# A four-layer image network: links of layer 0 on turns of their own, the scan's rows in bands, batch-norm statistics inside layer 2

## The chip, the cores and the metric

The program runs on one core of a Trainium2 chip. That core has four compute engines, each with its own in-order queue of instructions: PE (TensorE, matrix products into PSUM), DVE (VectorE), ACT (ScalarE) and POOL (GpSimd). A fifth queue, SP, issues every DMA of this kernel. The metric is the device time of one execution in microseconds; smaller is better. The profile shows, for PE, the clock that was granted as a share of the full one.

## The reference

Input `x` has 16 images of 64 x 64 positions and 256 channels, in float32. Four layers follow one another, each `x = x + layer(gn(x))`, where `gn` normalises each of 32 groups of 8 channels over an image. Layers 2 and 3 are involutions (weights made from the pixel, applied to its 3x3 or 7x7 surroundings); the change doesn't touch what they compute. Layers 0 and 1 are these:

```python
# layer 0: linear attention, 8 heads of 32
q, k, v = split(x @ Wqkv)
q = softmax(q, over the 32 of a head) / sqrt(32)
k = softmax(k, over all 4096 positions)
context = einsum('bdnh,benh->bdeh', k, v / 4096)
out = layernorm(einsum('bdeh,bdnh->benh', context, q) @ Wout + bout)

# layer 1: channel gate, then two spatial gates
xc = x * sigmoid(fc(mean(x)) + fc(max(x)))       # per image and channel
m  = mean of xc over channels, per position
y  = s6(m)         # h = exp(delta*A)*h + delta*m*B, y = sum(h*C), over 4096 positions
s  = conv7x7([mean, max of xc over channels])
x2 = xc * sigmoid(y) + xc * sigmoid(s)
out = relu((x2 - mean) / sqrt(var + eps) * gamma + beta)   # mean, var over all images
```

The last line is a batch norm: its mean and variance need all 16 images before any of them can go on.

## The kernel before

**Stages.** One function, `network`, writes the whole program; Python loops unroll all of it. Stage a is layer 0, with the gate and the channel maps of layer 1. Stage s holds layer 1's convolution, its scan, and its batch-norm statistics. Stage b is layer 2, stage c layer 3. Each stage opens pools of SBUF and PSUM buffers and closes them at its end, so that a later stage's buffers can lie where an earlier stage's were. Outside of a `manual_schedule` block, the framework chooses the order of instructions on each engine by the dependences and by the order in which they were written; inside one, they stay as written.

**Stage a.** It runs 256 turns and 16 more at the end. An image has 16 turns: two halves of four heads (`hf`), each with 8 chunks of 512 positions (`t`). In each turn, `attended` makes queries (pq, L280), and keys and values (pkv, L292), of one chunk on PE; ACT copies them out (L284, L301). Three kinds of further work are spread over the turns:

- For the half that was finished before: the context. `context` is a Python generator. Each `yield` ends a link, and `step()`, called five times in a turn, starts the next link. Links: the maximum of the keys over positions on DVE (mx, L311-L315), its transpose pk on PE (L331) and the diagonal matrix of it; the product pb that spreads the maximum over all partitions (L338), the subtraction on DVE (L341) and the exponential on ACT (L344); the product of keys and values pctx (L350, 128 small matmuls), scaled into cs.
- For the same half: the queries' softmax. `weighted` is a second generator. For each of two halves of the chunk range: maximum on DVE (L387), subtraction on POOL (L375), exponential on ACT (L380), sum and reciprocal on DVE (L383, L384), multiplication on POOL (L375 again). `output` then transposes queries (qT, L405), multiplies them with cs (po, L408) and transposes the result back (L409). `PARTS` says which of the eight outputs belong to which turn.
- For the image before: in the second half's turns, `projected0` (py, L423; bias, L428; squares on ACT, L432; the power on POOL, L435; transposes pt, L444; maxima and statistics, L451, L455). After an image's last chunk comes the gate `gate1`: group norm statistics (pg L134, pv L151, DVE L146-L148, the variance plus eps L93, POOL's power L94), av (L466-L469), ph (L477), hr and hs, pgate (L487), the sigmoid on ACT (L491), and the scale `ab` (L492-L494). `mapped` then takes the image two before: xm is scaled (ACT L172, DVE L175), transposed (px, L505) and reduced over channels on DVE (L509, L510).
- For the next image: `entered` takes statistics of the input (L246), and `norm0` makes from them the scale with which xn is normalised (ACT L165, DVE L166), half of the channels on each engine. A turn's pq needs its xn.

`norm0` and `gate1` are generators too, appended to `chains` in the turn in which their last chunk is done. py, pkv and px share a PSUM pool of two buffers; small products (pk, pb, pctx, pg, pv, ph, pgate) share one buffer.

**Stage s.** After the convolution (psc, L691), `r3` holds three rows for each image: delta, delta*m*m and delta*m, side by side for all images. The scan goes over 8 chunks of 512 positions with two groups of 8 images (16 steps). `rowed` transposes r3 (pr, L726) and ACT copies it (L731), for each chunk. `decayed` makes pa (L736): two matmuls over all 48 rows, against tables in which the rows of other images and of the other product are zero. ACT takes the exponential of one (L740), DVE scans (L749), PE sums over states (pys, L760), DVE writes y (L767, L768). Then the sigmoids are added to `fac`, which is transposed to rows (L777), copied to `held` (L778) and written to DRAM (`fac_d`, L779).

The statistics follow (L784-L800): for each of 128 tiles, x1 is loaded (L789, four buffers), PE spreads a row of `held` over the partitions (pf, L792), DVE computes z = (x1 - mean) * pf with a running sum (L797), and ACT squares z with a running sum (L801). Some 25 small operations (L805-L831) make `bnp` and rescale `ab`.

**Stage b.** Constants are loaded (L909-L917, and `folded` at L849), the padded tile `pad` is cleared on POOL (L923). Then a `manual_schedule` block runs 152 turns. In turns 0 to 127, `end_of_layer1` takes 512 positions of an image: x1 and pf are loaded again (L939, pf with a broadcast from `fac_d`), z is computed again (L970), ACT applies the norm and relu (L976), POOL adds x1 (L980), the sum is stored for later turns (L1208) and ACT squares it (L987). The projections start at turn 13, the involution at turn 21. A turn's loads are issued one turn ahead, and ahead of the stores of the turn before.

Of the kernel before, what the change touches and what calls it, by code (L numbers as in the profile page):

```python
# [15 lines left out]
P = 128  # L16
# [20 lines left out]
def network(ctx: ExitStack, tc: tile.TileContext, a: dict, out: bass.AP):  # L37
# [142 lines left out]
    with ExitStack() as st:  # L180
# [59 lines left out]
        def entered(i, ch):  # L240

            if ch == 0:
                st0[i] = wk.tile([P, 2, NCH, 6], F32, tag="st0", name="st0")
            xin = loaded.pop(("xin", i, ch))
            for h in range(2):
                nc.vector.bn_stats(st0[i][:, h, ch, :], xin[:, h])  # L246
            if i >= 2:
                stores.extend(halo.pop(0) for _ in range(min(3, len(halo))))
            if ch == NCH - 1:
                chains.append(norm0(i))  # L250
# [8 lines left out]
        normal = {}  # L259

# [57 lines left out]
        def context(i, hf):  # L318


            _, ka, va = qkv[i, hf]
            kf = ka.rearrange("p j d h -> p j (d h)")
            t = tree_max(
                lambda t: [kf[:, 8 * k : 8 * k + 8, :] for k in range(4)]
                + [t.rearrange("p (j e) -> p j e", e=P)],
                lambda t: [(t[:, 0:n], t[:, n : 2 * n]) for n in (512, 256, 128)],
            )
            yield
            yield
            pk = sm.tile([P, CT], F32, tag="sm", name="pk")  # L330
            nc.tensor.transpose(pk[:, 0:P], t[:, 0:P], ident)  # L331
            kmc = small.tile([P, 1], F32, tag="kmc", name="kmc")
            nc.vector.tensor_reduce(kmc, pk[:, 0:P], AX.X, ALU.max)
            diag = wk.tile([P, P], F32, tag="diag", name="diag")
            nc.vector.tensor_scalar(diag, ident, kmc, None, ALU.mult)
            yield
            pb = sm.tile([P, CT], F32, tag="sm", name="pb")
            nc.tensor.matmul(pb[:, 0:P], lhsT=ones, rhs=diag, start=True, stop=True)  # L338
            for jh in range(2):
                part = kf[:, jh * 16 : (jh + 1) * 16, :]  # L340
                nc.vector.tensor_tensor(  # L341
                    part, part, pb[:, 0:P].unsqueeze(1).broadcast_to([P, 16, P]), ALU.subtract
                )
                nc.scalar.activation(part, part, AF.Exp)  # L344
            yield
            yield
            pctx = sm.tile([P, CT], F32, tag="sm", name="pctx")
            for j in range(32):
                for h in range(4):
                    nc.tensor.matmul(  # L350
                        pctx[32 * h : 32 * h + 32, 0 : NB + 1],
                        lhsT=ka[:, j, :, h], rhs=va[:, j, :, h],
                        start=(j == 0), stop=(j == 31),
                    )
            rz = small.tile([P, 1], F32, tag="rz", name="rz")
            nc.vector.reciprocal(rz, pctx[:, NB : NB + 1])

            cs = wk.tile([P, P], F32, tag="cs", name="cs")
            nc.vector.scalar_tensor_tensor(
                cs.rearrange("p (h e) -> p h e", h=4),  # L360
                pctx[:, 0:NB].unsqueeze(1).broadcast_to([P, 4, NB]), rz,
                hmask.rearrange("p (h e) -> p h e", h=4), ALU.mult, ALU.mult,
            )
            ctx_m[i, hf] = cs

        def weighted(i, hf):
# [11 lines left out]

            def exponential(k):
                nc.scalar.activation(qa[:, halves[k]], qa[:, halves[k]], AF.Exp)  # L380
# [5 lines left out]
            for k in range(2):  # L386
                nc.vector.tensor_reduce(mq[:, halves[k]], qa[:, halves[k]], AX.X, ALU.max)  # L387
                scaled(k, mq, ALU.subtract)
                yield
            exponential(0)  # L390
            yield
            summed(0)
            exponential(1)
            yield
            scaled(0, mq, ALU.mult)
            summed(1)
            yield
            scaled(1, mq, ALU.mult)
            om[i, hf] = slots.tile([P, P, NB], F32, tag="slot", name="o")
# [13 lines left out]
        def projected0(i, ch):  # L413
# [45 lines left out]
            if ch == NCH - 1:  # L459
                chains.append(gate1(i))  # L460
# [83 lines left out]
        PARTS = ((), (), (), (0,), (1,), (2, 3), (4, 5), (6, 7))  # L544
        PARTS_LAST = ((), (), (), (0, 1), (2, 3, 4), (5, 6, 7), (), ())

# [7 lines left out]
        for ch in range(NCH):  # L554
# [4 lines left out]
            stores.clear()  # L559
        while chains:  # L560
# [4 lines left out]
        for n in range(LAST + 16):  # L565
# [6 lines left out]
            if t == 0 and 0 <= before[0] < NI:  # L572
                chains.append(context(*before))
            if t == 1 and 0 <= before[0] < NI:
                chains.append(weighted(*before))
# [55 lines left out]
    with ExitStack() as st:  # L631
# [4 lines left out]
        sm = st.enter_context(tc.tile_pool(name="s_sm", bufs=2, space=PSUM))  # L636

# [6 lines left out]
        bng = sconst("bng", [P, 2], a["bn_gamma"])  # L644
        bnb = sconst("bnb", [P, 2], a["bn_beta"])
# [4 lines left out]
        wrow = sconst("wrow", [3 * NI, NG, 2, P], a["wrow"].rearrange("k (g n s) -> k g n s", g=NG, n=2))  # L650
        wout = sconst("wout", [P, 16], a["wstate"])
        mv2 = sconst("mv2", [P, 2, 2, NI])
# [56 lines left out]
        r3 = sconst("r3", [P, NB, NI, 3])  # L709
        rd, rdmm, rdm = (r3[:, :, :, k].rearrange("p d i -> p i d") for k in range(3))  # L710
        nc.vector.scalar_tensor_tensor(rd, z, 0.0, az, ALU.max, ALU.add)
        nc.vector.tensor_tensor(rdm, rd, m, ALU.mult)
        nc.vector.tensor_tensor(rdmm, rdm, m, ALU.mult)
# [5 lines left out]
        with tc.manual_schedule():  # L719
# [3 lines left out]
            def rowed(ch):  # L723
                pr = tr.tile([P, CT], F32, tag="tr", name="pr")
                for q in range(4):
                    nc.tensor.transpose(  # L726
                        pr[0 : 3 * NI, q * P : (q + 1) * P],
                        r3[:, ch * 4 + q].rearrange("p i k -> p (i k)"), ident,
                    )
                rows[ch] = wk.tile([3 * NI, CT], F32, tag="rows", name="rows", bufs=2)  # L730
                nc.scalar.copy(rows[ch], pr[0 : 3 * NI, :])  # L731

            def decayed(ch, g):
                pa = mm.tile([P, 2, CT], F32, tag="mm", name="pa")
                for k in range(2):
                    nc.tensor.matmul(  # L736
                        pa[:, k], lhsT=wrow[:, g, k, :], rhs=rows[ch], start=True, stop=True
# [42 lines left out]
        facr = fac_d.rearrange("(i c) t -> i (c t)", i=NI)  # L780
# [3 lines left out]
        tot = sconst("tot", [P, 2, 2, NI, NCH])  # L784
        for i in range(NI):
            for ch in range(NCH):
                tk = slice(ch * CT, (ch + 1) * CT)
                x1 = wk.tile([P, 2, CT], F32, tag="x1", name="x1", bufs=4)
                nc.sync.dma_start(out=x1, in_=x1_d[i, :, :, tk].rearrange("h p t -> p h t"))  # L789
                pf = tr.tile([P, CT], F32, tag="tr", name="pf")  # L790
                row = i * NCH + ch
                nc.tensor.matmul(  # L792
                    pf, lhsT=ident[0:n, row : row + 1].broadcast_to([n, P]), rhs=held[0:n],
                    start=True, stop=True,
                )
                for h in range(2):
                    nc.vector.scalar_tensor_tensor(  # L797
                        x1[:, h], x1[:, h], ngm1[:, i, h : h + 1], pf, ALU.add, ALU.mult,
                        accum_out=tot[:, 0, h, i, ch : ch + 1],
                    )  # L800
                    nc.scalar.activation(  # L801
                        x1[:, h], x1[:, h], AF.Square, accum_out=tot[:, 1, h, i, ch : ch + 1]
                    )
        for k in range(2):
            nc.vector.tensor_reduce(mv2[:, :, k, :], tot[:, k], AX.X, ALU.add)  # L805
        nc.vector.tensor_scalar(mv2, mv2, 1.0 / NT, None, ALU.mult)
        sqm = sconst("sqm", [P, 2, NI])
        nc.vector.tensor_tensor(sqm, mv2[:, :, 0, :], mv2[:, :, 0, :], ALU.mult)
        nc.vector.tensor_tensor(mv2[:, :, 1, :], mv2[:, :, 1, :], sqm, ALU.subtract)
        for h in range(2):  # L810
            gate = ab[:, 0, :, h]
            nc.vector.tensor_tensor(mv2[:, h, 0], mv2[:, h, 0], gate, ALU.mult)
            nc.vector.tensor_tensor(mv2[:, h, 1], mv2[:, h, 1], gate, ALU.mult)
            nc.vector.tensor_tensor(mv2[:, h, 1], mv2[:, h, 1], gate, ALU.mult)


        mvb = sconst("mvb", [P, 2, 2])
        nc.vector.tensor_reduce(mvb[:, 0, :], mv2[:, :, 0, :], AX.X, ALU.add)
        nc.vector.tensor_scalar(mvb[:, 0, :], mvb[:, 0, :], 1.0 / NI, None, ALU.mult)
        dev = mv2[:, :, 0, :]  # L820
        for h in range(2):
            nc.vector.tensor_scalar(dev[:, h], dev[:, h], mvb[:, 0, h : h + 1], None, ALU.subtract)
        nc.vector.tensor_tensor(dev, dev, dev, ALU.mult)
        nc.vector.tensor_tensor(dev, dev, mv2[:, :, 1, :], ALU.add)
        nc.vector.tensor_reduce(mvb[:, 1, :], dev, AX.X, ALU.add)
# [832 lines left out]
```

## Time and profile before

| | |
|---|---|
| three runs | 8206.47, 8218.75 and 8226.33 us, median 8218.75 |
| the profiled execution | 8218.71 us |
| its span, first to last instruction | 8216.8 us |
| mean granted PE clock | 0.918 |
| PE, DVE, ACT, POOL busy | 6831.6, 5933.2, 4827.7, 3044.1 us |
| last pq of stage a starts | 2883.4 us |
| first psc of stage s starts | 3059.4 us |
| first and last scan start | 3074.5 and 3167.4 us |
| first statistic (L797) starts, last ends | 3176.5 and 3407.6 us |
| layer 2, turns 0, 1 and 8: z (L970) starts | 3416.8, 3429.8 and 3468.4 us |

A line of the profile by instruction gives: start and length in us, engine, line of the program, operation, output and inputs, sizes, and in brackets how long the engine had stood idle and what ended that. In a line by stretch, the pairs are busy time and number of instructions of PE, of PE's weight loads, DVE, ACT and POOL, then the granted clock, the busy share of the DMA engines and what they moved in GB/s. A matmul in float32 is two passes, each its own record. Turn lengths below are taken between the first pq of one turn and of the next; images 3 to 14 agree within some 4 us in 184.

### The profile page before, as it was taken

The numbers are of one execution on the slowest core, as the hardware profiler recorded it, in microseconds if no ns is written. First come the engines' busy times: TensorE is split into PE (matmuls) and PEld (weight loads), VectorE is DVE, ScalarE is ACT, GpSimd is POOL, SyncE is SP. The second block draws the span as 40 slices with busy tenths as digits, with TensorE's granted clock in tenths as the row PEclk, the third lists the DMA queues.
The fourth block names the chain that finished last, engine by engine and source line by source line (L and its number), as shares of the span: only waits on it lengthen the run. The fifth ranks groups of instructions, "written<-read, shape, count | busy, mean of one in ns | idle before, by whom it ended". The sixth has DMA issues, their size and how long they took to land. (4 is left out here: it accounts for less than half of the span.)

```text
span 8216.8 us, 213294 instructions
## 1 busy us (share of the span) xinstructions
PE 6831.6 (83%) x88348; PEld 5191.9 (63%) x88348; DVE 5933.2 (72%) x7071; ACT 4827.7 (59%) x11136; POOL 3044.1 (37%) x2154
## 2 busy tenths in 40 slices
PE   7888888888888867478888888888588888888897
PEld 5666666666666643156666666666477777777776
DVE  6787778787777775679999999999644444444444
ACT  3555555555555544676776767665455555555554
POOL 1222222222222210167888888887411212111112
PEclk9999999999999977798888888888799999999999
DMA  7644444344333334766777777775588888888887
GB/s 225 188 142 138 139 136 141 131 145 144 124 113 118 116 102 151 249 221 231 268 262 261 271 252 267 262 258 200 176 257 258 259 258 256 261 259 257 255 256 245
DMA packets 1079706, 1695.53 MB, mean 206 GB/s; under 512 B 136785, under 2 KB 682914, under 8 KB 1077586
## 3 DMA queue, kind: packets, MB, share of 16 engines
q1 hardware_dynamic: 1078738, 1681.89, 63.1%
q8 instruction: 696, 11.40, 0.6%
q14 instruction: 272, 2.23, 0.1%
HBM read 1234.54 MB, written 469.76 MB: 207 GB/s over the span
## 5 line engine op out<-in xcount | busy, mean ns | idle before, releaser
L1102 DVE TENSOR_TENSOR pd<-xs,pw 128x4608 f32<-128x4608 f32 x256 | 1261.2, 4946 | 1.4 <-ACT xs L1083 1.4
L1376 PE MATMUL pk<-rt,span 64*128 64x176 f32 x12288 | 1177.9, 328 | 52.6 <-issue 47.9
L1386 ACT ACTIVATE wm<-pk,spanb 128x176 f32<-128x176 f32 x2560 | 845.7, 424 | 573.4 <-PE pk L1376 570.3
L1115 POOL TENSOR_TENSOR pd<-pd 128x2048 f32<-128x2048 f32 (+2 forms) x384 | 1071.6, 2791 | 173.1 <-DVE pd L1102 82.7
L1462 POOL TENSOR_TENSOR ex<-ex,rx 128x192 f32<-128x192 f32 (+2 forms) x768 | 436.6, 570 | 1820.6 <-DVE ex L1455 1232.1
L1376 PEld LDWEIGHTS pk<-rt,span 64*128 64x128 f32 x12288 | 967.8, 191 | 132.8 <-issue 75.9
L1455 DVE SCALAR_TENSOR_TENSOR ex<-pa,msk,ex 128x192 f32<-128x192 f32 x704 | 294.3, 418 | 1006.5 <-ACT ex L1454 948.4
L292 PE MATMUL pkv<-wq,xn 128*128 128x256 f32 x4096 | 967.9, 382 | 14.4 <-ACT va L301 14.2
L1442 PE MATMUL pa<-wm,xw 126*32 126x48 f32 x45056 | 758.2, 214 | 220.9 <-issue 206.2
L375 POOL TENSOR_TENSOR qa<-qa,mq 128x1024 f32<-128x1024 f32 x256 | 507.4, 2005 | 1168.8 <-DVE mq L384 503.0
L1079 PE MATMUL pt<-ident,pad 128*128 128x128 f32 x4608 | 760.1, 327 | 214.8 <-ACT xs L1083 207.6
L1391 DVE TENSOR_TENSOR wm<-pk,spanb 128x704 f32<-128x704 f32 x896 | 794.2, 888 | 188.9 <-PE pk L1376 186.3
L292 PEld LDWEIGHTS pkv<-wq,xn 128*128 128x128 f32 x4096 | 771.3, 192 | 227.4 <-issue 101.1
L1442 PEld LDWEIGHTS pa<-wm,xw 126*32 126x32 f32 x45056 | 624.6, 111 | 403.1 <-issue 359.0
L1079 PEld LDWEIGHTS pt<-ident,pad 128*128 128x128 f32 x4608 | 623.6, 168 | 401.4 <-ACT xs L1083 265.5
L1083 ACT COPY xs<-pt 128x512 f32<-128x512 f32 x1152 | 608.0, 587 | 170.1 <-PE pt L1079 167.2
L1273 DVE TENSOR_REDUCE x<-pd 128x512 f32<-128x4608 f32 x128 | 634.0, 4953 | 4.4
L280 PE MATMUL pq<-xn,wq 128*128 128x512 f32 x1024 | 528.2, 631 | 91.2 <-DVE xn L166 74.0
L423 PE MATMUL py<-wo,o 128*128 128x256 f32 x2048 | 525.0, 412 | 31.4 <-DVE maps L510 27.6
L1454 ACT ACTIVATE ex<-pa,msk 128x192 f32<-128x192 f32 x704 | 299.2, 425 | 392.7 <-PE pa L1442 198.5
L423 PEld LDWEIGHTS py<-wo,o 128*128 128x128 f32 x2048 | 487.7, 310 | 63.9 <-issue 38.0
L1033 PE MATMUL px<-x2p,wis 128*128 128x512 f32 x1024 | 467.7, 599 | 12.8 <-DMA x2p<-x_d 8.1
(234 smaller groups left out, 11663.8 us busy)
## 6 DMA issues: line engine op xcount, KB each, us to landing
xw<-strips SPq DMA_DIRECT2D x1408, 256.0 KB
xn<-in_x SPq DMA_DIRECT2D x256, 512.0 KB
x_d<-x SPq DMA_DIRECT2D x256, 512.0 KB
strips<-cen SPq DMA_DIRECT2D x352, 256.0 KB
xin<-in_x SPq DMA_DIRECT2D x128, 512.0 KB
x<-in_x SPq DMA_DIRECT2D x128, 512.0 KB
xm<-x_d SPq DMA_DIRECT2D x128, 512.0 KB
x<-x_d SPq DMA_DIRECT2D x128, 512.0 KB
```

What stands on the lines that cost most here:

```text
L280: nc.tensor.matmul(pq, lhsT=wq[:, h, f0 : f0 + P], rhs=xn[:, h], start=(h == 0), stop=(h == 1),)
L292: nc.tensor.matmul(pkv[:, q], lhsT=xn[:, h, q * P : (q + 1) * P], rhs=wq[:, h, f0 + P : f0 + 384], start=(h == 0), stop=(h == 1),)
L423: nc.tensor.matmul(py[:, q, :], lhsT=om[i, hf][:, :, ch * 4 + q], rhs=wo[:, hf, :], start=(hf == 0), stop=(hf == 1),)
L1079: nc.tensor.transpose(pt[:, k, h * P : (h + 1) * P], lines[:, h, rc * 4 + e + k, 2 * j : 2 * j + P], ident,)
L1083: nc.scalar.copy(xs[:, e : e + 2, j, :], pt)
L1102: nc.vector.tensor_tensor(pd.rearrange("p r (g f) k -> p r g f k", f=16), run, pw.rearrange("p r (g k) -> p r g k", k=9).unsqueeze(3).broa ...
L1115: nc.gpsimd.tensor_tensor(pd[..., 0:n], pd[..., 0:n], pd[..., n : 2 * n], ALU.add)
L1273: nc.vector.tensor_reduce(x3[:, :, P:C], pd1, AX.X, ALU.add)
L1376: nc.tensor.matmul(pkv[:, b, m], lhsT=span[half, first + gg, s0 : s0 + P], rhs=rto[half, o // 4 * 2 + m, :], start=True, stop=True,)
L1386: nc.scalar.activation(dst[:, m // 2, m % 2], pkv[:, m // 2, m % 2], AF.Identity, bias=spanb[:, g0 + m : g0 + m + 1],)
L1391: nc.vector.tensor_tensor(dst, pkv, spanb[:, g0 : g0 + 4].rearrange("p (b m) -> p b m", b=2).unsqueeze(3).broadcast_to([P, 2, 2, NTL]), AL ...
L1442: nc.tensor.matmul(pav[p0 : p0 + 32, :, tj * TC : (tj + 1) * TC].rearrange("c g (w v) -> c g w v", v=2), lhsT=xw[0:TILE_IN, k, tj, 32 * q ...
```

## The change

Three parts. First, in layer 0, the links of `context` and `weighted` are no longer separated by a fixed number of `yield`s: a list says for each link at which step it runs, counted from the step in which its chain starts. `norm0` and `gate1` are put aside in `waiting` and start at turn 1 of the next half. `PARTS` leaves turn 3 without an output and gives turn 4 two. The last image's gate and the last half keep lists of their own.

```diff
@@ entered / projected0
-                chains.append(norm0(i))
+                waiting.append(norm0(i))
...
-                chains.append(gate1(i))
+                (waiting if i < NI - 1 else chains).append(gate1(i))
@@ new
+        def until(links):
+            at = 1
+            for step_no, link in links:
+                while at < step_no:
+                    yield
+                    at += 1
+                link()
@@ context: bodies of the links unchanged, each now a function
+            links = [maximum, diagonal, spread] + [
+                lambda jh=jh: exponential(jh) for jh in range(2)
+            ] + [product]
+            return until(zip(at, links))
@@ weighted
+            links = []
+            for f in (shifted, exponential, summed, lambda k: scaled(k, mq, ALU.mult)):
+                links += [lambda f=f, k=k: f(k) for k in range(2)]
+            order = sorted(range(8), key=lambda n: at[n])
+            return until([(at[n], links[n]) for n in order] + [(max(at), ended)])
@@ turns
-        PARTS = ((), (), (), (0,), (1,), (2, 3), (4, 5), (6, 7))
+        PARTS = ((), (), (), (), (0, 1), (2, 3), (4, 5), (6, 7))
+        CONTEXT, CONTEXT_LAST = (1, 5, 14, 14, 15, 19), (1, 3, 4, 4, 4, 7)
+        WEIGHTED, WEIGHTED_LAST = (1, 3, 5, 7, 11, 13, 12, 14), (1, 2, 3, 4, 4, 5, 5, 6)
...
-                chains.append(context(*before))
+                chains.append(context(*before, CONTEXT if n < LAST else CONTEXT_LAST))
             if t == 1 and 0 <= before[0] < NI:
-                chains.append(weighted(*before))
+                chains.append(weighted(*before, WEIGHTED if n < LAST else WEIGHTED_LAST))
+            if t == 1:
+                chains.extend(waiting)
+                waiting.clear()
```

In the old form the context's links ran at steps 1, 3, 4, 4, 4 and 6, and those of the queries at 1, 2, 3, 4, 4, 5, 5 and 6.

Second, the scan. `r3` becomes 128 columns wide for each block of positions: a band of 32 for each group of 8 images and each of the two products, cleared once and filled in part. Each matmul of pa reads its own band alone, 8 rows for the decay and 16 for the input.

```diff
+        r3 = pc.tile([P, NB, 2, 2, 32], F32, tag="r3", name="r3")
+        nc.gpsimd.memset(r3, 0.0)
...
-                        pr[0 : 3 * NI, q * P : (q + 1) * P],
-                        r3[:, ch * 4 + q].rearrange("p i k -> p (i k)"), ident,
+                        pr[:, q * P : (q + 1) * P],
+                        r3[:, ch * 4 + q].rearrange("p g k i -> p (g k i)"), ident,
...
+                    p0 = 64 * g + 32 * k
+                    band = slice(p0, p0 + 8 + 8 * k)
                     nc.tensor.matmul(
-                        pa[:, k], lhsT=wrow[:, g, k, :], rhs=rows[ch], start=True, stop=True
+                        pa[:, k], lhsT=wrow[band], rhs=rows[ch][band], start=True, stop=True
                     )
```

Third, the statistics leave stage s and become `batch_norm`, called first in stage b's `manual_schedule` block. It reads `held` back from `fac_d`, goes over images 1 to 15 and then image 0, and leaves image 0's x1 and z in the buffers of `xs` and `pd`, which layer 2 first uses at turn 20. Turns 0 to 7 of layer 2 then load nothing and compute no z. The tables for gamma and beta move to stage b's constants.

```diff
+        def batch_norm():
+            x1s = [spare(xs_p, [P, 6, 3, C], "xs") for _ in range(2)]
+            zs = [spare(pd_p, [P, 4, P, 9], "pd") for _ in range(2)]
...
+            nc.sync.dma_start(out=held, in_=fac_d)
+            todo = [(i, ch) for i in range(1, NI) for ch in range(NCH)]
+            todo += [(0, rc) for rc in range(NCH)]
+            def begin(k):
...
+                if i:
+                    tag = ("x3", "x2r")[k % 2]
+                    x1 = wk.tile([P, 2, CT], F32, tag=tag, name="x1", bufs=3)
...
+            for k in range(5):
+                begin(k)
+            for k, (i, ch) in enumerate(todo):
+                begin(k + 5)
...
@@ end_of_layer1
-            x1, pf = taken("x1"), taken("pf")
-            zs = [wk.tile([P, 2, 256], F32, tag="z", name="z", bufs=1), pf]
...
+            if i:
+                x1, pf = taken("x1"), taken("pf")
...
+            else:
+                x1, zs = (t.rearrange("p h (g t) -> p h g t", g=2) for t in kept.pop(rc))
@@ loads
-            if end:
+            if end and end[0]:
                 load_layer1(*end)
@@
         with tc.manual_schedule():
+            batch_norm()
             loads(0)
```

## The prediction

> **What bounds the kernel now.** I read first the busy times by stage, cut at each stage's first and last instruction.
>
> ```profile
> core 0: us, PE busy (x) PEld busy (x) DVE busy (x) ACT busy (x) POOL busy (x), PEclk, DMA share, GB/s
> 38.00:2884.00 2846.00, 2482.14 (x17611) 1887.91 (x17610) 2181.68 (x3213) 1627.15 (x2962) 643.24 (x426) 0.95 0.43 142
> 3059.00:3174.40 115.40, 105.16 (x249) 54.94 (x249) 33.11 (x69) 22.26 (x33) 0.00 (x0) 0.54 0.00 0
> 3174.40:3413.20 238.80, 156.54 (x256) 41.64 (x256) 184.21 (x537) 176.87 (x512) 0.70 (x2) 0.92 0.84 277
> 3413.20:3468.40 55.20, 0.00 (x0) 0.00 (x0) 15.49 (x25) 24.29 (x60) 28.04 (x18) 0.50 0.67 188
> ```
>
> Each line is a stretch, its length, each engine's busy time, the granted clock, the DMA engines' share and rate. Layer 0's 256 turns (line one) are 87% PE, with 364 us in which PE stands still. The scan (line two) is PE at 0.54 of its clock. Line three is the batch-norm statistics, with no engine full and DMA at 0.84; line four the first eight turns of layer 2. After 3468.4 us both programs have the same instructions in the same order on every engine, so only what lies before can change.
>
> Next, one image of layer 0 (16 turns, 183.4 us) by groups of turns: 0-2, 3-4, 5-7, 8-10, 11-15.
>
> ```profile
> 1417.60:1440.00 22.40, 19.07 (x72) 12.89 (x72) 22.40 (x32) 16.18 (x21) 6.54 (x4) 0.92 0.49 164
> 1440.00:1475.20 35.20, 22.23 (x341) 17.13 (x341) 29.29 (x58) 12.97 (x17) 9.34 (x7) 0.90 0.42 134
> 1475.20:1499.10 23.90, 23.59 (x98) 16.11 (x97) 19.55 (x26) 11.23 (x15) 1.81 (x1) 1.00 0.59 200
> 1499.10:1547.80 48.70, 42.52 (x417) 35.58 (x416) 40.84 (x46) 29.59 (x58) 17.20 (x12) 0.93 0.30 102
> 1547.80:1601.00 53.20, 52.06 (x222) 40.40 (x222) 32.36 (x56) 35.78 (x86) 6.93 (x7) 1.00 0.40 136
> ```
>
> Turns 5-7 and 11-15 are PE without a gap. PE loses 13.0 us in turns 3-4, 6.2 in 8-10, 3.3 in 0-2. PE's timeline says to whom:
>
> ```profile
> 1445.07 1.12 PE L280 MATMUL pq<-xn,wq 128*128 128x512 f32 x2 [3.90 <-DVE xn L166]
> 1450.93 3.27 PE L350 MATMUL pctx<-va,ka 128*32 128x33 f32 x183 [3.49 <-DVE isq L93]
> 1464.08 1.09 PE L505 MATMUL px<-ident,xm 128*128 128x128 f32 x8 [2.26 <-ACT xm L172]
> 1503.00 5.53 PE L423 MATMUL py<-wo,o 128*128 128x256 f32 x16 [2.02 <-DVE maps L510]
> 1517.32 0.33 PE L331 MATMUL pk<-ident,mx 128*128 128x128 f32 x1 [2.97 <-DVE mx L315]
> 1544.27 3.72 PE L423 MATMUL py<-wo,o 128*128 128x256 f32 x16
> ```
>
> It waits for VectorE each time (px for xm, whose scale comes from the gate). A stall costs twice: the same 16 passes took 5.53 us after one and 3.72 at the end of turn 10.
>
> **Layer 0, part by part.** No operation is added or removed; links move. In the order of instructions of the two built programs, turns 0-1 stand as before on all engines, except that PE's last item in turn 1 is the gate's pg instead of the contexts' pb.
>
> Half 0 (turns 0-7), on the clock above. Turn 2 starts at 1433.1 (before 1433.66) and PE runs pq and pkv to 1439.8. VectorE: kmc, diag and small ones to 1433.3, two query sums of 2.27 with a reciprocal of 0.54 and small ones to 1438.8. Then xn of turn 3 (0.54): it waits for POOL's multiply, as rows of L166 took 1.58 and of L175 2.14 beside one; 1440.4. Behind it the norm's dev, pv on PE to 1441.4, the variance at 1442. POOL's power stands between two multiplies of 1.95: 1443.7; the two av scalars wait out the second: 1446.2. ph, hr, two transposes (0.68), hs, pgate: 1448.5, where L487 was at 1459.8. PE then does pq of turn 4 (1.9) and pb, to 1450.8. The key subtraction, now here, is 2.24 twice on VectorE (1455.5), its exponential 1.91 on ACT; xm follows at 1456.0. What PE has left of turns 3-4 is px 1.0, pkv 3.7, the rest of pctx 4.2, px 1.0, pkv 1.85, po 1.9, pkv 1.85, px 1.0, together 16.7: turn 5 starts at 1472.7 against 1475.2, and takes 7.8 as turn 6 does, not 8.4. That is -3.1. PE has two gaps here, 1442.4-1446.3 and 1451-1456; if the passes after them run as slowly as the 5.53 row, 1.6 comes back. I take -1.5 (bounds +2, if every small VectorE item is held by POOL once more, and -5).
>
> Half 1. Turn 8 keeps its order and its 2.0 us wait. In turn 9 the order py x6, pk, py x2 puts 2.8 us of PE work where PE waited 2.97 for mx: mx is ready at 1516.4, py ends its six at 1516.8. That removes the wait and the slow py behind it (4.98 for 14 passes, 3.3 at the later rate): -4.6. In turn 10 pv stands second on PE, ahead of py, pkv, pt and pb; on VectorE it is behind the query sum (2.27), xn, a reciprocal and the maxima of x (0.69 each, up to 2.39 beside POOL): 1527.5, PE is there at 1526.0, so +1.6. pctx goes from turn 10 to the end of turn 11: pb at 1537.9, subtractions done by 1544.2, exponentials 1546.8, PE arrives at 1547.6, so no wait; the x normalisation that waits behind the subtractions is needed only a turn later. Two outputs in turn 12 instead of one each in 11 and 12 are the same work. Sum -3; the walk through all items gives -1.8; I take -2.5 (bounds +2, -6).
>
> So -4.0 us an image, times 14 images that have all the work: -56. In images 0 and 1 three halves show pctx waiting inside a turn (turns of 13.1 and 12.0 us between ones of 5 to 8); with pctx two turns after pb I count 4 each: -12. The last 16 turns keep their steps. Layer 0: -68 (bounds +44, -166).
>
> The Trainium skill, "TensorE: Matmul & The Clock Gate", Part 1, speaks against this change: after about 3.4 us without work the clock is halved, and comes back only after some 3.4 us of work. By that rule both gaps of half 0 would cost the full 1.7 us each; the sum would be 8136 instead of 8112.
>
> **Scan.** Before, a step's pa is four passes over 48 rows:
>
> ```profile
> 3104.60 0.58 ACT L731 COPY rows<-pr 48x512 f32<-48x512 f32 x1 [2.09 <-PE pr L726]
> 3105.23 3.78 PE L736 MATMUL pa<-rows,wrow 48*128 48x512 f32 x4 [0.67 <-ACT rows L731]
> 3108.93 1.89 PE L760 MATMUL pys<-wout,hst 128*128 128x16 f32 x8
> 6501.59 2.06 PE L1376 MATMUL pk<-rt,span 64*128 64x176 f32 x24
> ```
>
> PE is the loop: pa 3.78 + pys 1.89, and every second step 1.6 more for pr and its copy; 12.65 a pair. After, the two matmuls of pa use rows in different bands (8 and 16 rows, 32 apart). The last line is the nearest row: layer 3 alternates two 64-row bands; 24 passes of 176 columns in 2.06 us, where one after another they would need 24 x 176 x 0.43/512 = 3.5. So bands run side by side. Then pa is two passes long, 2.1, and a pair 9.7: 8 x 2.95 = 23.6. VectorE's loop (pys 1.89, ysc 0.46, scan 1.27, waits 0.2) is 3.8, just under PE's 4.0. The wider transposes and the six half-sized rd operations add some 0.6; the memset of r3 (4096 columns; L923 took 7.58 for 8976) has idle POOL for cover and would cost 3.5 without. I take -23 (bounds 0, if they don't overlap, and -35).
>
> In layer 3 PE goes from 32-column to 64-row tiles without a gap: 48 passes of L1442 end at 6501.67, L1376 starts at 6501.59. The Trainium skill, "TensorEngine Tiling (Array Packing)", Key Properties, says that a change of tiling mode drains TensorE; pa and pys alternate, 32 changes. By the row that is nothing; by the rule, with the 0.2 us by which a pass of L736 (1.05) outlasts the start of the next (0.85 on) as an estimate, the sum would rise by 6.
>
> **Statistics.** These are the same 256 VectorE and 256 ACT operations. Three things move.
>
> ```profile
> DVE x L797 <- DMA x<-x_d: 33.5, 57, 1.8
> SPq L789 <- ACT x L801: 170.9, 124, 3.9
> DVE z L970 <- DMA pf<-fac_d: 32.1, 8, 5.2
> ```
>
> (Who waited for whom: total us, times, longest.) First, the start. Before, four tiles lay loaded and the first operation ran at 3176.5. After, SP issues 17 constants first (15 took 10.2 us at 3413-3423, so 11.5), then reads held back from DRAM, then x1, which lands 3.5 us after issue (L222 at 1512.06, used at 1515.4): 3190.5, +14. Second, the loop: 128 tiles in 231 us, 1.80 each, with VectorE at 1.44 and DMA at 0.84. SP waited 171 us for a free one of four buffers; now there are six. Bounds 1.87 a tile (281 GB/s, none preloaded) and 1.57 (DMA share 1.0 at that rate); I take 1.76: -6. Third, the end. The constants, the memset of pad and image 0's loads no longer stand between the last statistic and layer 2: the first relu comes 5.6 us after it (before 10.1), and turns 0-7 go by ACT at 2 x (0.81+0.19) + 2 x (0.70+0.19) = 3.8 instead of 6.4. Turn 8's loads stand on SP behind the store of turn 5, and pf takes 6.6 from issue; its z comes at about +36.5 against +60.8: -24. Sum -16 (bounds -40, and +2 if pf also lands 4 us later).
>
> **Sum.** Against the profiled execution, 8218.7 (span 8216.8 and 1.9 around it; the median is 8218.75): 8218.7 - 68 - 23 - 16 = 8112.
>
> **Rivals.** (1) The gate's chain takes the freed place: in half 0 it and the contexts, now one behind the other, eat what the order saves, and half 1's pv wait does the same; layer 0 stays. For it: PE idles 9 us in turns 3-4 by my own walk. Against: the gate is done 11 us earlier. 8218.7 - 39 = 8180. (2) PE's queue is held by the norms: pv stands ahead of 16 us of free PE work in turn 10, and ahead of all of turn 3. For it: VectorE items of 0.1 us took 1.9 (L148) and maxima 2.39 beside POOL. At 5 us more at each pv, an image is 10 - 4 = 6 longer: 8218.7 + 84 - 12 - 39 = 8252, slower. It decides from 4.8 us net an image. (3) Layer 0's gaps close: of 22.5 us lost an image only 11 stay, 14 x 11.5 = 161 and 12: 8218.7 - 173 - 39 = 8007. Against: VectorE has 29 of 35 us in turns 3-4. (4) Bands don't overlap: 8135, a variant of the forecast.
>
> **Numbers.** Forecast with (4) 0.48, own range 8060 to 8165; (1) 0.20; (2) 0.17; (3) 0.15. A measurement of this kernel tells about 0.2%, 16 us. The forecast, (3) and two thirds of (1) are faster: 0.76; the rest of (1) and a little of (2) within: 0.09; slower 0.15. The range 8010 to 8230 leaves out half of (3) and most of (2).
>
> **What would show it.** The turns: 3-4 at some 33 us instead of 35.2 and 8-11 at 57 instead of 59.2; pk without a wait, pv with one of about 1.6, pctx in turn 11 without one; clock in turns 8-10 above 0.93. A scan pair of 9.7 us, with pa near 2.1. First statistic 14 us after the copy of held, 1.76 a tile, relus 3.8 us apart. I am wrong if turn 3's pq or turn 10's pv waits over 5 us, if pa stays 3.8, or if anything after layer 2's turn 8 changes its length.

## The result, and the profile after

The changed kernel takes 8111.56 us (median of 4 runs, 8107.73 to 8118.0) beside 8220.52 for the kernel before (4 runs, 8206.47 to 8226.33): ratio 0.987, 95% interval 0.9856 to 0.9883. The forecast of 8112 us was met by luck, not by its own sum. The two profiled executions, cut at the same events:

| stretch (us) | before | changed | difference | forecast |
|---|---|---|---|---|
| first to last pq of layer 0 | 2847.3 | 2852.1 | +4.9 | -68 |
| last pq to first psc | 174.7 | 171.8 | -2.9 | 0 |
| first psc to first scan | 15.1 | 14.3 | -0.8 | (in -23) |
| first scan to end of the copy of held | 99.8 | 75.8 | -24.0 | -23 |
| from there to the first statistic | 2.2 | 17.1 | +14.9 | +14 |
| 128 tiles of statistics | 231.1 | 174.4 | -56.6 | -6 |
| last statistic to the relu of layer 2's turn 8 | 61.6 | 33.5 | -28.1 | -24 |
| from there to layer 3's first pk | 2455.9 | 2455.1 | -0.8 | 0 |
| layer 3 | 2291.7 | 2275.8 | -15.9 | 0 |

Layer 0 gave nothing, and the loop of the statistics gave nine times what was put down for it. The stretches of the changed kernel, with the columns of the prediction's first fence:

```profile
38.00:2888.50 2850.50, 2515.81 (x17611) 1918.69 (x17610) 2134.87 (x3212) 1629.48 (x2961) 636.88 (x426) 0.94 0.43 142
3060.40:3150.90 90.50, 78.27 (x248) 46.20 (x248) 31.84 (x69) 22.20 (x33) 0.00 (x0) 0.56 0.00 0
3150.90:3168.00 17.10, 2.08 (x3) 1.08 (x4) 1.91 (x8) 0.01 (x1) 8.12 (x2) 0.50 0.38 113
3168.00:3342.50 174.50, 143.13 (x270) 41.22 (x269) 172.42 (x513) 171.37 (x509) 0.00 (x0) 0.99 1.02 379
3342.50:3348.80 6.30, 0.00 (x0) 0.00 (x0) 4.27 (x24) 1.02 (x5) 0.70 (x1) 0.50 0.00 0
3348.80:3375.10 26.30, 0.00 (x0) 0.00 (x0) 0.02 (x1) 23.51 (x60) 19.93 (x16) 0.50 0.48 170
```

Layer 0: PE is busy 33.7 us longer than before at a clock of 0.94 instead of 0.95, in a stretch 4.5 us longer. What the new order took away in idle time (334.7 us instead of 363.9) came back as slow passes. The statistics (fourth line) are now VectorE 172 of 174.5 us and ACT 171, with the DMA engines at 379 GB/s instead of 277 to 282. Turns 0 to 7 of layer 2 (last line) are set by ACT, busy for 23.5 of 26.3 us.

One image of layer 0 in the changed kernel, by groups of turns 0-2, 3-4, 5-7, 8-11, 12-15:

```profile
1424.60:1445.10 20.50, 17.50 (x73) 12.16 (x72) 20.50 (x35) 14.81 (x20) 8.70 (x5) 1.00 0.50 179
1445.10:1482.70 37.60, 25.66 (x337) 19.11 (x336) 31.07 (x51) 16.82 (x21) 6.20 (x5) 0.82 0.42 141
1482.70:1506.00 23.30, 23.30 (x98) 16.17 (x97) 19.03 (x24) 9.09 (x13) 1.75 (x1) 1.00 0.54 181
1506.00:1566.50 60.50, 53.05 (x466) 44.64 (x465) 43.58 (x64) 38.64 (x78) 18.71 (x14) 0.94 0.38 123
1566.50:1609.90 43.40, 42.34 (x177) 32.15 (x176) 27.14 (x45) 27.05 (x65) 5.89 (x6) 1.00 0.33 110
```

Beside the image of the prediction, turns 0-2 are shorter by 2 and turns 3-4 longer by 2.4, at a clock of 0.82 where it was 0.90; turns 8-11 and 12-15 had been 59.2 and 42.7. That image was a short one in turns 3-4: on the mean of images 3 to 12 they went from 37.0 to 38.3 us, at 0.81 instead of 0.85. PE's timeline says why they got no shorter. First turns 3-4:

```profile
1447.25 0.38 PE L151 MATMUL pv<-gn_d,gmat 128*128 128x2 f32 x2 [1.14 <-DVE gn_d L148]
1452.32 0.40 PE L498 MATMUL ph<-av,w1T 128*16 128x2 f32 x4 [3.73 <-DVE av L490]
1453.82 1.01 PE L508 MATMUL pgate<-hs,w2T 16*128 16x1 f32 x4 [1.09 <-DVE hs L504]
1454.76 3.46 PE L290 MATMUL pq<-xn,wq 128*128 128x512 f32 x4
1458.06 0.39 PE L352 MATMUL pb<-diag,ones 128*128 128x128 f32 x2
1463.18 0.69 PE L368 MATMUL pctx<-va,ka 128*32 128x33 f32 x26 [4.74 <-DVE ka L358]
1463.80 1.97 PE L526 MATMUL px<-ident,xm 128*128 128x128 f32 x8
1465.56 4.84 PE L302 MATMUL pkv<-wq,xn 128*128 128x256 f32 x16
```

Read it as one chain: pv, ph and pgate of the gate, each after a wait for VectorE; only then pb, which shares their PSUM buffer; then the subtraction on VectorE and pctx. In the kernel before, the keys were ready at 1442.6 us (the end of ACT's exponentials), ahead of the gate's pv at 1446.9, and pctx, po and pq stood between the gate's products (pctx from 1450.93 on):

```profile
1440.71 1.91 ACT L344 ACTIVATE ka<-ka 128x2048 f32<-128x2048 f32 x1
1446.85 0.58 PE L151 MATMUL pv<-gn_d,gmat 128*128 128x2 f32 x2 [0.66 <-DVE gn_d L148]
1457.11 0.24 PE L477 MATMUL ph<-av,w1T 128*16 128x2 f32 x4 [0.79 <-DVE cs L359]
1457.28 1.12 PE L408 MATMUL po<-qT,cs 128*128 128x512 f32 x2
1459.19 0.60 PE L487 MATMUL pgate<-hs,w2T 16*128 16x1 f32 x4
```

Now the two chains follow each other, and PE has only pq to put between. The passes behind these waits run slowly: pq 3.46 us (1.88 elsewhere), px 1.97 (1.04), pkv 4.84 (3.62). Then turns 8-11:

```profile
1510.99 5.55 PE L444 MATMUL py<-wo,o 128*128 128x256 f32 x16 [3.09 <-ACT va L311]
1524.23 0.27 PE L344 MATMUL pk<-ident,mx 128*128 128x128 f32 x1
1533.96 0.38 PE L151 MATMUL pv<-gn_d,gmat 128*128 128x2 f32 x2 [1.38 <-DVE gn_d L148]
1535.29 5.55 PE L444 MATMUL py<-wo,o 128*128 128x256 f32 x16 [0.95 <-ACT va L311]
1555.90 3.40 PE L368 MATMUL pctx<-va,ka 128*32 128x33 f32 x188
1561.34 1.41 PE L368 MATMUL pctx<-va,ka 128*32 128x33 f32 x68 [2.04 <-issue]
```

pk no longer waits and pctx doesn't wait for its keys, as forecast (the 2.04 us in its middle have no cause that the profile shows; such a hole, 1.19 us, was there before). In turn 8 py waits 3.09 us, where it had waited 2.02. The wait for pv is 1.38, near the 1.6 forecast, but py behind it waits again and takes 5.55 instead of 3.72.

### The profile page after: what moved, and what is told of

Its sections match the earlier page's. It is cut to its first block, busy times and chain, and to the rows that moved or that the text cites. A ratio compares the mean times of both kernels' runs of the same rounds, so it can differ in the third digit from the quotient of the medians.

```text
span 8106.8 us, 213269 instructions
## 1 busy us (share of the span) xinstructions
PE 6834.8 (84%) x88364; PEld 5225.4 (64%) x88364; DVE 5862.4 (72%) x7058; ACT 4824.8 (60%) x11136; POOL 3041.1 (38%) x2155
## 4 chain that ended last, share of the span: by engine, by line
PE 48%; DVE 27%; issue 10%; DMA 6%; ACT 6%; POOL 2%; SPq 1%; DVEq 0%; POOLq 0%; ACTq 0%
PE pk L1468 13%; DVE pd L1193 8%; PE pa L1534 8%; PE pkv L302 6%; DVE x L1365 5%; PE py L444 5%; PE pq L290 3%; PE pt L1170 2%; PE pctx L368 2%; PE px L1124 2%; PE pr L1435 2%; DVE mq L403 1%; PE po L429 1%; DMA xn<-in_x 1%; DVE x L472 1%
## 5 line engine op out<-in xcount | busy, mean ns | idle before, releaser
L290 PE MATMUL pq<-xn,wq 128*128 128x512 f32 x1024 | 533.0, 637 | 35.9 <-ACT xn L165 23.4
```

Of the source, the lines that this page charges most:

```text
L290: nc.tensor.matmul(pq, lhsT=wq[:, h, f0 : f0 + P], rhs=xn[:, h], start=(h == 0), stop=(h == 1),)
```

## The experiments

Twelve kernels. Those of layer 0 are judged by the time from the first to the last pq in the profile, because whole times carry the differences of layer 3. A table of these stands behind e12. The twelve ran on four chips (e1 to e4, e5 to e8, e9 and e10, e11 and e12), and the changed kernel's own layer 0 did not run on the last three. The same old layer 0 took 2847.3 us in the first profile and 2857.7 and 2859.1 in e1 and e4, so differences of some 10 us between chips mean nothing here.

**e1: all but layer 0's part**

```diff
-                waiting.append(norm0(i))
+                chains.append(norm0(i))
...
-                (waiting if i < NI - 1 else chains).append(gate1(i))
+                chains.append(gate1(i))
...
@@ and PARTS, CONTEXT and WEIGHTED as in the diff of e5 below
```

> The changed kernel with layer 0 as it was before: norms and gate start at once, contexts at steps 1, 3, 4, 4, 4, 6, queries at 1, 2, 3, 4, 4, 5, 5, 6, outputs from turn 3. The scan's bands and the moved statistics stay. Theory A (layer 0's part gained nothing: its last pq starts 4.3 us later and the next stage 1.4 us later than before): 8111.6 - 1.4 = 8110, within 8100 to 8120, and the last pq back at about 2883. Rival (the prediction's term of 68 us is there and something else in the trace hides it): 8180.

Ratio 0.9891, interval 0.9861 to 0.9921; first to last pq 2857.7 us, and 2859.1 and 2860.6 in e2 and e3, which have the new layer 0 and ran on the same chip. So layer 0's part is worth nothing that can be measured; theory A holds. The absolute numbers of the expectation were missed (8148.3 us for 8110): layer 0 took some 10 us more than in the first profiles, in e4 too, and layer 3 took 19 more (2295.1 for 2275.8). Beside the kernel before on its own chip e1 is 89.5 us shorter, where the changed kernel was 109.0.

**e2 and e4: four buffers after, six before**

```diff
@@ e2, in the changed kernel
-                    tag = ("x3", "x2r")[k % 2]
-                    x1 = wk.tile([P, 2, CT], F32, tag=tag, name="x1", bufs=3)
+                    tag = ("x1", "xc")[k % 2]
+                    x1 = wk.tile([P, 2, CT], F32, tag=tag, name="x1", bufs=2)
...
-            for k in range(5):
+            for k in range(3):
...
-                begin(k + 5)
+                begin(k + 3)
@@ e4, in the kernel before
-                x1 = wk.tile([P, 2, CT], F32, tag="x1", name="x1", bufs=4)
+                x1 = wk.tile([P, 2, CT], F32, tag="x1", name="x1", bufs=6)
```

> The changed kernel with four buffers in place of six for x1 in the statistics, three tiles ahead instead of five. Theory D (the loop fell from 1.80 to 1.36 us a tile because six loads may be on their way instead of four): the loop goes back to about 1.80 us a tile, 231 us, and the time to 8111.6 + 56 = 8168. Rival P (the order written out by hand, the other places of the buffers, or the stage without stores beside it made the loads faster): the loop stays at 1.36 us a tile, time 8112.

> The kernel before with six buffers for x1 in its statistics instead of four, and nothing else. Theory D: the loop takes about 1.36 us a tile, 174 us instead of 231, and the time is 8220.5 - 57 = 8164. Rival P: 1.80 us a tile, 8220.

The loop's stretch in e2, then in e4, columns as above:

```profile
3174.70:3405.00 230.30, 151.52 (x271) 45.50 (x269) 179.58 (x512) 175.70 (x509) 0.00 (x0) 0.94 0.88 288
```

```profile
3184.60:3360.80 176.20, 143.23 (x254) 37.49 (x253) 173.34 (x512) 172.32 (x510) 0.00 (x0) 1.00 1.00 364
```

230.3 us with four buffers in the new place, 176.2 with six in the old one: the number of buffers does it and the move nothing. The times go the same way, less clearly: 8204.5 and 8187.6 us (one run each) beside 8237.8 for the kernel before on that chip, so 33 and 50 us less where the expectations come to 52 and 57.

**e3: products of the scan on shared rows**

```diff
-                    band = slice(p0, p0 + 8 + 8 * k)
+                    band = slice(64 * g, 64 * g + 8 + 40 * k)
```

> The changed kernel, but the second matmul of pa reads 48 rows from the first one's band on, so that the two share rows of TensorE; the first band's table is added into the input, so the output is not the reference's. Theory (the two products ran side by side because their rows lie in bands apart): pa goes from 2.08 us back to about 3.8, a pair of scan steps from 9.2 to about 12.4 us, time 8111.6 + 25 = 8137. Rival (fewer rows made each pass shorter): the first product stays short, pa about 3.0, a pair about 11, 8126.

PE in the changed kernel, then in e3:

```profile
3102.34 2.08 PE L770 MATMUL pa<-rows,wrow 8*128 8x512 f32 x4
3104.34 1.89 PE L794 MATMUL pys<-wout,hst 128*128 128x16 f32 x8
3106.07 1.09 PE L758 MATMUL pr<-ident,r 128*128 128x128 f32 x4
3107.84 2.07 PE L770 MATMUL pa<-rows,wrow 8*128 8x512 f32 x4 [0.68 <-ACT rows L763]
```

```profile
3137.69 4.07 PE L770 MATMUL pa<-rows,wrow 8*128 8x512 f32 x4
3139.69 2.07 PE L770 MATMUL pa<-rows,wrow 48*128 48x512 f32 x2
```

Four passes in 2.08 us in bands apart, 4.07 with a shared band, where two passes of 48 rows alone take 2.07. The two passes of 8 rows ahead of them take as long (3137.69 to 3139.69). A pass of few rows is as long as one of many; side by side is the gain. A scan step was 6.56 us in e3, 4.59 in the changed kernel and 6.19 before: 105.3 us for the stretch against 75.8. The time was 8173.9 us in one run, where 8137 was expected; the changed kernel has no run on that chip to set beside it.

**e5 and e6: one half of layer 0's change each**

```diff
@@ e5
-        PARTS = ((), (), (), (), (0, 1), (2, 3), (4, 5), (6, 7))
+        PARTS = ((), (), (), (0,), (1,), (2, 3), (4, 5), (6, 7))
-        CONTEXT, CONTEXT_LAST = (1, 5, 14, 14, 15, 19), (1, 3, 4, 4, 4, 7)
-        WEIGHTED, WEIGHTED_LAST = (1, 3, 5, 7, 11, 13, 12, 14), (1, 2, 3, 4, 4, 5, 5, 6)
+        CONTEXT, CONTEXT_LAST = (1, 3, 4, 4, 4, 6), (1, 3, 4, 4, 4, 7)
+        WEIGHTED, WEIGHTED_LAST = (1, 2, 3, 4, 4, 5, 5, 6), (1, 2, 3, 4, 4, 5, 5, 6)
@@ e6
-                waiting.append(norm0(i))
+                chains.append(norm0(i))
...
-                (waiting if i < NI - 1 else chains).append(gate1(i))
+                chains.append(gate1(i))
```

> The changed kernel with only the norms and the gate put off to turn 1; contexts, queries and outputs at the steps of before. Read from the first to the last pq of layer 0 (before 2847.3, changed 2852.1 us on the first chip; 2857.7 to 2860.6 in four kernels on the second). Theory S (the gate's chain and the context's, each with holes on PE, stand one behind the other in the changed kernel; if only one is moved, the other's products fill its holes): 2 to 4 us less an image, about 2815. Theory V (VectorE sets the first turns, busy 20.5 of 20.5 us in turns 0 to 2 and 31.1 of 37.6 in 3 and 4, so the order of links is worth little): 2845 to 2865.

> The changed kernel with the norms and the gate started at once as before; contexts, queries and outputs at the new steps. Theory S: the gate is done before the context's product, whose chain then fills the holes: 2 to 4 us less an image, about 2815 from first to last pq. Theory V: 2845 to 2865.

2814.0 us with the norms put off alone, 2776.8 with the links moved alone, where both together gave 2852 to 2861. Theory S holds, in e6 by more than its 2815, and theory V's 2845 to 2865 falls: the links alone, with the same work, are worth 75 to 84 us. Turns 2-4 of e6 on PE:

```profile
1397.91 0.28 PE L151 MATMUL pv<-gn_d,gmat 128*128 128x2 f32 x2
1402.55 0.40 PE L498 MATMUL ph<-av,w1T 128*16 128x2 f32 x4 [0.81 <-DVE av L490]
1405.72 0.60 PE L508 MATMUL pgate<-hs,w2T 16*128 16x1 f32 x4 [1.40 <-DVE hs L504]
1406.95 0.80 PE L352 MATMUL pb<-diag,ones 128*128 128x128 f32 x2 [0.63 <-ACT gate L512]
1415.32 0.69 PE L368 MATMUL pctx<-va,ka 128*32 128x33 f32 x26 [4.42 <-ACT ka L362]
```

pv now stands among the passes of pkv without a wait, ph waits 0.8 instead of 3.7, and pb comes 6.2 us after the start of turn 3 (1400.7) instead of 13.0 (1445.1). In the second half no pv stands ahead of py in turn 10, so that turn takes 14.0 us on the mean instead of 18.0. The remaining wait, pctx for the keys, is nearly the same as in the changed kernel.

**e7 and e8: two more ways to loosen turns 3-4**

```diff
@@ e7
-            if at(i - 2) and (t >= 2 if hf == 0 else t < 2):
-                todo.append(("xm", i - 2, (t - 2) % NCH))
+            if at(i - 2) and (t >= 4 if hf == 0 else t < 4):
+                todo.append(("xm", i - 2, (t - 4) % NCH))
@@ e8
-                got["pb"] = sm.tile([P, CT], F32, tag="sm", name="pb")
+                got["pb"] = tr.tile([P, CT], F32, tag="tr", name="pb")
...
-        CONTEXT, CONTEXT_LAST = (1, 5, 14, 14, 15, 19), (1, 3, 4, 4, 4, 7)
+        CONTEXT, CONTEXT_LAST = (1, 5, 8, 9, 11, 19), (1, 3, 4, 4, 4, 7)
```

> The changed kernel with the channel maps of an image two turns later (turns 4 to 7 of the first half and 0 to 3 of the second). It takes two px and two pairs of reductions (2.4 us of VectorE each) out of turns 2 to 4. Theory V: 4.8 us less in the first half, some 2 us more in the second, where PE is 88% busy: 2.8 us an image, about 2815 from first to last pq. Theory S (px waits only 0.2 us an image, the holes belong to gate and context): 2845 to 2865.

> The changed kernel with pb in the PSUM pool of three buffers that pq, pt and po use, instead of the one buffer that pk, pb and the products of norms and gate share, and the context's links at steps 1, 5, 8, 9, 11 and 19, so that pb and the subtractions need not wait for the gate. Theory S: the wait of pctx for the keys (6.3 us an image in turns 3 and 4) and the slow passes behind it go: 4 to 6 us less an image, about 2785 from first to last pq. Theory V: at most 1 us an image, 2845 to 2865.

e7: 2815.2, theory V's number, and not the 2845 to 2865 of theory S: VectorE's work in turns 2-4 counts beside the order. But it is not V's by its parts: turns 3-4 lose 9.4 us, not 4.8, and turns 8-11 gain 6.2, where py waits 8.2 us an image. e8: 2798.1, short of the 2785 of theory S and far below the 2845 of theory V. On the mean pctx waits 2.1 us an image instead of 6.3, but pq now waits 2.9 for xn in its place. Buffer and steps were changed together, so no run says what each of them gave.

**e9 to e12: the links of e6 with e8's buffer, with later maps, with both, and alone**

```diff
@@ e9: e6 with the two edits of e8
@@ e10: e6 with
-            if at(i - 2) and (t >= 2 if hf == 0 else t < 2):
-                todo.append(("xm", i - 2, (t - 2) % NCH))
+            if at(i - 2):
+                late = ((), (), (), (0,), (1,), (2,), (3,), (4, 5)) if hf == 0 else ((6,), (7,))
+                todo += [("xm", i - 2, k) for k in (late[t] if t < len(late) else ())]
@@ e11: e9 with the edit of e10; e12: e6 once more
```

> The version with only the links moved (norms and gate at once; 2776.8 us from first to last pq), and pb in the PSUM pool of three buffers with the context's links at steps 1, 5, 8, 9, 11 and 19. Theory S (the wait of pctx for the keys, 5.7 us an image in turns 3 and 4, goes as it fell by 4 in the version with pb in its own buffer): 3 to 4 us less an image, about 2725 from first to last pq, time some 50 below that version's 8076. Rival (subtractions and norms now meet in turns 0 to 2, where VectorE has no time left): 2765 to 2790.

> The version with only the links moved, and the channel maps of an image in turns 3 to 7 with two in turn 7, instead of 2 to 7. It takes one px and one pair of reductions out of turns 2 to 4 and leaves the second half's number of them as it is. Theory S with V: half of what two turns gave in the first half (9 us), so 3 to 4 us less an image, about 2725. Rival (the doubled map slips into turn 8, ahead of py, and py waits as it did with maps two turns later, 6 us more there): 2770 to 2800.

> The two last versions in one: only the links moved, pb in the pool of three PSUM buffers with the context's links at steps 1, 5, 8, 9, 11 and 19, maps in turns 3 to 7 with two in turn 7. Theory S: what is left in turns 3 and 4 is pgate's wait of 4.0 us in the one and pctx's of 4.2 in the other, which exclude one another, so some 3 us an image less than the better of them: about 2645 from first to last pq, a ratio to the kernel before near 0.965. Rival (one wait takes the other's place, as when norms and links were moved together): 2680 to 2700, ratio 0.968 to 0.971.

> The version with only the links moved, norms and gate at once as before (its single run stood at 8076.0 against 8228.7, 0.9815), once more for an interval. Theory S: ratio 0.980 to 0.984, clear of the changed kernel's 0.987, interval 0.9856 to 0.9883. If the two intervals meet, the 80 us of layer 0 were not there in each execution.

e9 2697.5 and e10 2686.5, both better than expected. e11 was wrong: 2732.0, above its rival too. In turns 3-4 pgate waits 3.4 us for VectorE there, pctx 1.8, and the clock is 0.88 on the mean (0.95 in e10). That one loosening again got in the other's way is how these waits read; it wasn't tested, nor whether other steps would make them add up. e12 gave 0.9794, interval 0.9775 to 0.9813, a little below the expected 0.980 to 0.984 and clear of the changed kernel's; from first to last pq it took 2774.7 us, beside 2776.8 for e6 on another chip.

Mean time of an image's groups of turns (images 3 to 12), and layer 0 from first to last pq:

| | 0-2 | 3-4 | 5-7 | 8-11 | 12-15 | layer 0 | time beside the kernel before |
|---|---|---|---|---|---|---|---|
| before | 21.5 | 37.0 | 23.8 | 59.6 | 42.6 | 2847.3 | |
| changed | 21.1 | 38.3 | 23.3 | 60.0 | 43.3 | 2852.1 | 0.987 (0.9856 to 0.9883) |
| e1, old links | 21.7 | 37.9 | 24.0 | 60.0 | 42.8 | 2857.7 | 0.9891 (0.9861 to 0.9921) |
| e5, norms put off | 21.7 | 33.8 | 23.3 | 60.8 | 42.7 | 2814.0 | 8105.8 to 8228.7, one run |
| e6, links (layer 0 in e12: 2774.7) | 22.3 | 34.2 | 23.4 | 56.7 | 43.6 | 2776.8 | e12: 0.9794 (0.9775 to 0.9813) |
| e7, maps 2 later | 22.0 | 28.9 | 23.3 | 66.2 | 43.4 | 2815.2 | 8111.6 to 8228.7, one run |
| e8, pb apart | 21.7 | 32.1 | 23.3 | 60.9 | 43.7 | 2798.1 | 8083.1 to 8228.7, one run |
| e9 | 22.2 | 27.9 | 23.5 | 57.6 | 43.4 | 2697.5 | 7992.5 to 8239.4, one run |
| e10 | 23.1 | 25.3 | 23.4 | 58.4 | 43.6 | 2686.5 | 7979.2 to 8239.4, one run |
| e11 | 22.2 | 28.7 | 23.4 | 59.0 | 43.3 | 2732.0 | 0.9736 (0.9718 to 0.9753) |

So versions that beat both kernels exist: e11 is 2.6% faster than the kernel before, and e10 is likely better still (7979.2 beside 8239.4 is 0.968), with one run only. Turns 3-4 of one image in e10:

```profile
1368.00:1392.40 24.40, 20.21 (x328) 15.19 (x328) 22.22 (x38) 15.88 (x19) 4.34 (x4) 1.00 0.33 109
```

24.4 us instead of 37.6, in this image at full clock (0.95 on the mean of images 3 to 12). VectorE's work there fell from 31.1 to 22.2 us, and rose in the groups behind it, where VectorE isn't full: 20.8 of 23.4 us instead of 19.0 in turns 5-7, 49.2 of 59.9 instead of 43.6 in 8-11.

## Why the prediction was right, and where it was not

**Layer 0: the term of -68 failed, and rival (1) happened.** The chain was foreseen well. Counted from the start of turn 2 (1439.8 here, 1433.1 in the walk), pv came at 7.4 us (forecast 8.3), pgate at 14.0 (15.4) and px at 24.0 (22.9). The step that failed is "What PE has left of turns 3-4 is ... together 16.7" (its terms add up to 16.5). It took 18.9: px and the pkv behind it ran slowly (2.1 us in all), and 1.2 us of idle time stood among the later pkv; the rest was a little shorter. With the 1.1 by which px was late, turn 5 started at 42.9 us after turn 2, forecast 39.6, and 41.5 before. The gain that the walk saw, 1.9 us by then, was smaller than the 3.3 by which turn 5 came late. "1.6 comes back" was the right thing to count and too small: 1.6 behind the first wait and 2.2 behind the second. In the second half, turns 8-9 fell from 28.5 to 25.5 us on the mean of images 3 to 14, less than the -4.6 of pk; py waits longer in turn 8 (3.2 us on the mean instead of 2.0). Turns 10-11 rose from 31.0 to 34.4, where +1.6 had been taken for pv: its wait was mis-sized by what it does to py behind it, 0.95 idle and 1.8 of slow passes. (In e6, where no pv stands there, py waits 0.1.) The signs named for layer 0, 33 us for turns 3-4 and 57 for 8-11, failed with it: 38.3 and 60.0 on the mean. e5 and e6 show rival (1)'s mechanism, since either half of the change alone gains. Images 0 and 1, credited with -12, took 279.1 us instead of 273.8.

The comparison with the Trainium skill, "TensorE: Matmul & The Clock Gate", Part 1, went to the skill in the first half. The 1.7 us estimated from it for each of two waits is near the 1.6 and 2.2 measured. That some 3.4 us without work are needed before the clock is halved is not what the second half shows:

```profile
1531.60:1535.30 3.70, 1.38 (x7) 0.46 (x5) 3.70 (x13) 1.92 (x5) 2.29 (x3) 1.00 0.74 254
1535.30:1540.70 5.40, 5.40 (x17) 4.72 (x18) 2.59 (x6) 1.45 (x3) 2.71 (x3) 0.68 0.73 214
```

Two waits of 1.38 and 0.95, 2.3 us in 3.7, left py a granted clock of 0.68; before the change, one wait of 2.02 had been enough for a py of 5.53.

**Scan: right, and by its reason.** pa took 2.08 us (forecast 2.1), a pair of steps 9.2 (9.7), the stretch -24.0, and e3 is the proof. The rule of the Trainium skill, "TensorEngine Tiling (Array Packing)", Key Properties, that a change of tiling mode drains TensorE, was to add an estimated 6 us. The stretch shows none of them, and they had no place in the difference: pa and pys alternated as often in the kernel before. A change isn't free in either kernel. pys starts 0.98 us after the last pass of pa before (3107.95 to 3108.93) and 0.99 after the change (3103.35 to 3104.34), where the later passes of pa in the kernel before follow each other every 0.85.

**Statistics: the start and the end right (+14.9 for +14, -28.1 for -24), the loop mis-sized (-56.6 for -6).** At the end the relus came 3.2 us apart, not 3.8. In the loop, the failed step is the lower bound "1.57 (DMA share 1.0 at that rate)". It took the time that the DMA engines spent on a byte as fixed. With more loads on their way the same bytes took less: 65.0 MB at a share of 0.855 of 230.5 us before, 66.1 MB at 1.02 of 174 after, so 3.0 and 2.7 us for each MB. The buffers' round would have told it from the trace of before. Four buffers at 1.80 us a tile are 7.2 us, of which VectorE and ACT held a tile for 2.2 (3251.26 to 3253.44), so a load needed 5.0:

```profile
3251.26 0.75 DVE L797 SCALAR_TENSOR_TENSOR x<-x,ngm,pf 128x512 f32<-128x512 f32 x1 [0.72 <-DMA x<-x_d]
3253.25 0.19 ACT L801 ACTIVATION_READ_ACCUMULATOR x<-x 128x1 f32 x1
```

Six buffers at the engines' own 1.35 leave 8.1 - 2.2 = 5.9, enough if more loads on their way don't make each one 0.9 us longer, and the loop goes to VectorE. What VectorE still waited for in the changed loop:

```profile
DVE x L981 <- PE pf L973: 2.9, 1, 2.9
DVE x L981 <- DMA x<-x_d: 1.4, 3, 0.6
```

1.4 us for loads, where it had been 33.5.

**After turn 8** nothing changed its length up to layer 3. Layer 3 was 15.9 us shorter in the one execution, with the same instructions. In the profiles of the twelve experiments it took 2275.2 to 2314.2 us, whether layer 0 was old or new, but most of that lies between chips: on one chip it differed by 11.4 us at most. There, e4 with the old place of the statistics took 2303.5 and e1 to e3 with the new one 2295.1 to 2306.5. That points to chance and not to the change, but it isn't shown: the other stages of the two profiles add up to -93 us, the medians of four runs differ by 109, and where the rest comes from stays open. The forecast came out right because +73 in layer 0 met -51 in the loop, -4 at the end of the statistics and -16 in layer 3.

## What to carry to other kernels

Two moves that each take a wait away can cancel, when each chain had been filling the other's holes: run each alone before both. Price a deeper prefetch by the round of one buffer (buffers times the time of a tile, less what the engines hold it), not by the busy share of the DMA engines. And count for every wait of PE the slow passes behind it; they were nearly as large as the wait in some rows here (1.8 us behind 2.02).

## What was not expected of the hardware

- A share of DMA time is no ceiling: 0.86 at 282 GB/s became 1.02 at 379 GB/s with two more loads on their way. In e4, where nothing else was changed, it became 1.00 at 364.
- The clock fell behind waits of 2.0 us (py, 5.53 us in the kernel before) and of 1.38 and 0.95 us close together (5.55), with 3.72 us as the length at full clock.
- Layer 3, with the same instructions on every engine, differed by up to 39 us between profiles from different chips, and by 3 to 11 on one chip in the experiments (15.9 in the first two profiles). A gain of that size has to be read from its own stage.
